# Two decoder layers on one core: layer norms applied by ScalarE, layer 1's weight products made at the start, and a planner with a priority for every operation

## The chip, the cores and the metric

The kernel runs on one core of a Trainium2 chip. A core has five engines with queues of their own: TensorE (PE in the profile; its weight loads are shown apart as PEld), VectorE (DVE), ScalarE (ACT), GpSimd (POOL) and SyncE (SP), which here issues all DMAs. Every engine takes its instructions strictly in the order in which the program lists them; a wait at the head of a queue holds everything behind it.

The metric is the device time of one execution in microseconds (us), lower is better. The time before is 2389.19 us, the median of three runs (2387.06 to 2392.53).

## The reference

The input is `x` of 64 x 64 x 256 in float32 (4096 tokens of width 256, in 64 sequences of 64) and a context `ctx` of the same shape. Two layers of three blocks each are applied, each block to a layer norm of `x`, and its result is added to `x`:

```python
x = x + L0_attn(layernorm(x), ...)      # 16 heads of 128, 4 key heads, norm of q and k, rotary, causal
x = x + L0_xattn(layernorm(x), ctx, ctx) # 32 small heads of 8 channels, no causal mask
x = x + L0_ffn(layernorm(x), ...)       # dense layer plus one of 8 rank-16 experts
x = x + L1_attn(layernorm(x), ...)      # 16 heads of 16, one key head
x = x + L1_xattn(layernorm(x), ctx, ...) # 16 heads of 128, q and k normed by their rms over 2048
x = x + L1_ffn(layernorm(x), ...)       # gated, with 8-bit rounding of inputs and weights
```

Products that need more than half precision are made from a high and a low float16 part of each operand, in three matmuls (high x high, high x low, low x high).

## The kernel before

**Tiles and groups.** Tokens are worked on in 16 groups of 256 (`GT`). A group's `xt` is a tile of 128 partitions x 2 x 256. In phase a, a group goes through layer 0: `l0_attn`, `l0_xattn`, `l0_ffn`, and is stored to DRAM (`mid`); in phase b it is loaded again and goes through layer 1: `l1_attn`, `l1_xattn`, `l1_ffn`. Several groups are in flight at once, and the first groups of phase b overlap the last ones of phase a.

**How the order is made.** The functions don't emit instructions. They record operations with `s.o(engine, cost, reads, writes, fn)`, or with `s.alt`, where one of several engines may be taken. `Sched.plan` then simulates the engines with the recorded costs and picks, one by one, the operation to place next: among those that can start earliest (within `EPS`), the one with the smallest due time. A due time is the time at which the operation would run if its group ran alone, stretched and spaced by `PACE`, plus an offset by the name of the tile that it writes (`LEAD`). `tmin` is an earliest time, `after` adds a dependence, `WINDOW` limits how many groups of each phase are in flight, `SPACE` spaces the score matmuls of cross attention. Tiles come from pools (`COUNTS`): 8 PSUM banks (`B`), 67 tiles of 2 KB per partition (`k2`), 6 of 4 KB (`k4`) and so on; an operation is placed only when its buffers are free. The list so made is emitted, and the chip then runs each engine's part in that order, whatever the real durations are.

**Layer norm** (`layer_norm`, L530 to L548). DVE takes mean and variance (`ln_st`, `ln_mv`), POOL adds the epsilon and a scale and raises to the power -1/2 (`ln_rs`), and DVE applies it to each of the two halves of 256 columns as (x - mean) * rs, into `xh`. The factor `XS` = 16 is folded into rs. There are six per group, 96 in all.

**Layer 0's cross attention** takes `xh` times 16; `stack_rows` (L949) splits it into high and low parts scaled by 4/16 (ACT L955, DVE L956), stores them to DRAM and reads them back in another arrangement into `Q`, a part of a fixed tile named `ovl`. Score matmuls (`xs_ps` L1009, `xt_ps` L1043) work on 32 rows each; ACT takes the exponentials (`xpt` L1050), and PE multiplies by the values (`xo_ps` L1059); `xot_ps` (L1071) and `yo` (L1087) turn the result back.

**Setup for layer 1's cross attention** is recorded after phase a's group 1 with `tmin` = 150 us (in `net`), so it lies amid phase a. `gram_setup` (L1326), called for the q and for the k weights, makes W transposed times W in eight pieces of 256 rows: for each piece and each half of the columns, PE writes its own bank `g_ps` (L1343; the bias product in one column, L1345), and DVE adds the bank to `g_G` (L1350). `value_out_setup` (L1375) multiplies value and output weights of each head into `n_ps` (L1392), stores them to DRAM, finds a scale over all of them, loads them again, splits them into high and low and stores those. `l1_xattn_load` (L1484) loads the split weights (`x1wki`, `x1wq`, `x1wn`, 32 tiles of 2 KB) for phase b; it gives three of eight weights a dependence on layer 0's attention of group 14, and the other five on that of group 15. `l1_attn_setup` is recorded with the first setups, with `tmin` = 70 us.

**Layer 1's cross attention** makes its norms from the gram matrix (`gy_ps`), the projections `qk_ps` in `proj2` (L412 to L414), scores `s_ps` (L1632), values `vn_ps` (L1511) and the output `acc` (L1534).

## Time and profile before

| | us |
|---|---|
| median of three runs | 2389.19 |
| profiled execution, its own time | 2390.41 |
| profiled execution, span of the page | 2388.5 |
| PE busy | 2169.8 |
| DVE busy | 1948.4 |
| POOL busy | 1630.4 |
| ACT busy | 1516.3 |

The mean granted TensorE clock is 0.961 of full speed. The span counts from the first to the last instruction. A busy share is an average over stages that differ: the page also gives each engine's busy share in forty slices, with the TensorE clock in each, and those are to be read before the averages. In a row of the groups of instructions stand the line, the engine, the operation, what is written and read, the shapes and the count; then the busy time in us, the mean duration of one in ns, and the engine's idle time just before them with what ended it. Matmuls overlap one another, so the mean duration of one is longer than the time that it adds. A row of waits gives who waited for whom, the total in us, how often, and the longest.

### The profile page before, as it was taken

The numbers are of one execution on the slowest core, as the hardware profiler recorded it, in microseconds if no ns is written. First come the engines' busy times: TensorE is split into PE (matmuls) and PEld (weight loads), VectorE is DVE, ScalarE is ACT, GpSimd is POOL, SyncE is SP. The second block draws the span as 40 slices with busy tenths as digits, with TensorE's granted clock in tenths as the row PEclk, the third lists the DMA queues.
The fourth block names the chain that finished last, engine by engine and source line by source line (L and its number), as shares of the span: only waits on it lengthen the run. The fifth ranks groups of instructions, "written<-read, shape, count | busy, mean of one in ns | idle before, by whom it ended". The sixth has DMA issues, their size and how long they took to land. (4 is left out here: it accounts for less than half of the span.)

```text
span 2388.5 us, 69732 instructions
## 1 busy us (share of the span) xinstructions
PE 2169.8 (91%) x28232; PEld 1701.9 (71%) x28232; DVE 1948.4 (82%) x4532; ACT 1516.3 (63%) x2843; POOL 1630.4 (68%) x1572
## 2 busy tenths in 40 slices
PE   3499999888999898898878999999999999999996
PEld 2387666655566565665544779898999898899995
DVE  7768788898797889898988867887888888888767
ACT  6475666877878676777557565565556565566542
POOL 5899668777787577767645466767777666666632
PEclk9699999999999998999977999999999999999997
DMA  5243234444355333433464353343444334444321
GB/s 182 74 88 91 59 83 107 125 129 103 87 136 136 108 92 83 129 97 80 111 158 108 57 118 72 76 80 73 86 82 80 76 76 81 81 86 77 59 42 28
DMA packets 484323, 220.83 MB, mean 92 GB/s; under 512 B 340568, under 2 KB 463384, under 8 KB 484000
## 3 DMA queue, kind: packets, MB, share of 16 engines
q1 hardware_dynamic: 484000, 216.37, 39.9%
q8 instruction: 222, 3.64, 0.6%
q14 instruction: 101, 0.83, 0.1%
HBM read 89.06 MB, written 34.64 MB: 52 GB/s over the span
## 5 line engine op out<-in xcount | busy, mean ns | idle before, releaser
L1050 ACT ACTIVATE xpt<-xt_ps,xes 128x512 f32<-128x512 f32 x512 | 313.2, 698 | 75.5 <-PE xt_ps L1043 71.7
L1511 PE MATMUL vn_ps<-x1wn,cTs 128*64 128x256 f16 x6144 | 354.1, 274 | 0.0
L1511 PEld LDWEIGHTS <-cTs 128*64 128x64 f16 x6144 | 332.1, 110 | 8.4 <-issue 6.2
L1016 DVE TENSOR_REDUCE xmx<-xs_ps 128x2 f32<-128x512 f32 x512 | 317.2, 679 | 18.1 <-PE xs_ps L1009 17.4
L1518 DVE SCALAR_TENSOR_TENSOR vn<-vn_ps,vn 128x512 f16<-128x512 f32 x256 | 174.5, 684 | 96.9 <-ACT vn L1516 96.4
L1516 ACT ACTIVATE vn<-vn_ps 128x512 f16<-128x512 f32 x256 | 151.9, 595 | 159.3 <-PE vn_ps L1511 157.5
L604 POOL TENSOR_TENSOR s<-s,sm_mx 128x1024 f32<-128x1024 f32 x96 | 184.7, 1924 | 78.8 <-DVE sm_mx L603 71.4
L633 POOL TENSOR_TENSOR phl<-s,phl 128x512 f16<-128x512 f32 x192 | 223.6, 1176 | 12.3 <-ACT phl L632 10.3
L630 POOL TENSOR_TENSOR s<-s,sm_sm 128x512 f32<-128x512 f32 x192 | 199.5, 1056 | 4.7 <-POOL sm_sm L623 0.3
L1059 PE MATMUL xo_ps<-xpt,xve 128*32 128x256 f32 x2048 | 165.0, 414 | 7.1 <-DVE s L1291 4.9
L815 POOL TENSOR_TENSOR qu<-qu,sw 128x512 f32<-128x512 f32 x128 | 165.5, 1304 | 2.0
L813 POOL TENSOR_TENSOR sw<-sw,rp0s 128x512 f32<-128x512 f32 x128 | 165.3, 1304 | 2.2 <-ACT sq L811 1.6
L810 ACT COPY sw<-q_ps 64x512 f32<-64x512 f32 x256 | 148.0, 580 | 28.1 <-PE q_ps L414 18.8
L632 ACT CAST phl<-s 128x512 f16<-128x512 f32 x192 | 118.2, 622 | 73.7 <-POOL s L630 70.8
L1761 POOL TENSOR_TENSOR gu<-gu 128x704 f32<-128x704 f32 x32 | 55.0, 1721 | 138.2 <-ACT sig L1759 129.9
L1620 ACT ACTIVATE k<-qk_ps,x1kb 128x256 f32<-128x256 f32 x242 | 101.4, 471 | 72.6 <-PE qk_ps L414 67.3
L412 PE MATMUL q_ps<-xT,l0w 128*128 128x256 f16 x512 | 139.8, 273 | 3.7 <-ACT sw L810 1.8
L412 PE MATMUL acc<-l0w,ohl 128*128 128x256 f16 x512 | 141.7, 277 | 0.6 <-ACT sw L810 0.2
L413 PE MATMUL acc<-l0w,ohl 128*128 128x256 f16 x512 | 141.4, 276 | 0.0
L414 PE MATMUL acc<-l0w,ohl 128*128 128x256 f16 x512 | 141.3, 276 | 0.0
L412 PE MATMUL qk_ps<-cTs,x1wki 128*128 128x256 f16 x512 | 140.3, 274 | 0.0
L412 PE MATMUL qk_ps<-xT,x1wq 128*128 128x256 f16 x512 | 139.7, 273 | 0.2 <-DVE xmx L1016 0.2
(414 smaller groups left out, 6666.4 us busy)
## 6 DMA issues: line engine op xcount, KB each, us to landing
ovl<-hl_d SPq DMA_DIRECT2D x96, 128.0 KB
vx<-vt SPq DMA_DIRECT2D x64, 128.0 KB
ctx<-in_ctx_dram SPq DMA_DIRECT2D x32, 256.0 KB
hl_d<-hl SPq DMA_DIRECT2D x64, 128.0 KB
wd<-w_hl SPq DMA_DIRECT2D x32, 256.0 KB
q1st<-q_d SPq DMA_DIRECT2D x128, 64.0 KB
xt<-in_x_dram SPq DMA_DIRECT2D x16, 256.0 KB
ctx_a<-in_ctx_dram SPq DMA_DIRECT2D x8, 512.0 KB
```

What stands on the lines that cost most here:

```text
L412: nc.tensor.matmul(out, lh, rh, start=(st and i == 0), stop=False, **kw)
L604: s.o("POOL", 1900, [mx], [s1], lambda m, t: nc.gpsimd.tensor_tensor(t, t, bc(m, 2, 64), ALU.subtract))
L630: s.o("POOL", 1030, [sm], [s1.sub(j)], lambda m, t, h=h: nc.gpsimd.tensor_tensor(t[:, h], t[:, h], bc(m[:, h], 2, 64), ALU.mult))
L633: s.alt([("POOL", c_pool(482), lambda t, _, p, h=h: nc.gpsimd.tensor_tensor(pl(p, 1), t[:, h], pl(p, 0), ALU.subtract)), ("DVE", c_dves(51 ...
L813: s.o("POOL", 1225, [sg], [sw], lambda t, w: nc.gpsimd.tensor_tensor(v(w), v(w), bc(t, 1, 8), ALU.mult))
L815: ("POOL", 1225, lambda w, d: nc.gpsimd.tensor_tensor(view(d), view(d), w, ALU.add))], [sw], [dt])
L1016: nc.vector.tensor_reduce(m[:, h, bs % 4, :], p, AX.X, ALU.max))
L1050: nc.scalar.activation(t, p, AF.Exp, scale=a))
L1059: nc.tensor.matmul(o[32 * hh:32 * hh + 32, hs, :], v[:, n, a:a + 32], r[hh][:, n, :], start=(n == 0 and hs == 0), stop=(n == 1), skip_grou ...
L1511: nc.tensor.matmul(r[-1][64 * h:64 * h + 64, p, :], x[:, b // 2, a, k, t], w.part(r, c, 2 * (2 * p + h) + k), start=(n == 0), stop=(n == 5))
L1516: nc.scalar.activation(v(t), p, AF.Copy, scale=2.0 ** -15))
L1518: nc.vector.scalar_tensor_tensor(v(l), p, 2.0 ** -15, v(h), ALU.mult, ALU.subtract))
```

## The change

The change has these parts.

1. `layer_norm`: POOL makes -mean * rs for each half (`ln_nb`), and ACT applies the norm as x * rs + nb, in place of DVE.
2. Layer 0's cross attention asks for its norm times 4, so that `stack_rows` splits it without a scale: a plain copy on ACT or DVE, and a subtraction on POOL or DVE.
3. `gram_setup` accumulates all eight pieces in two PSUM banks, computes the second half's columns 128 to 256 only, and reads the banks once at the end. Its pieces, and the value-out products (split off into `value_out_products`), get earliest times from 5 us on, 3 us apart, in place of 150 us on, 15 us apart.
4. `l1_attn_setup` moves to the setups recorded after group 1, with `tmin` = 150 us.
5. `l1_xattn_load`: the eight weights depend on layer 0's attention of groups 12, 12, 13, 14, 15, 15, 15, 15.
6. The planner: an offset for every operation of a group by its place (`FINE`), a penalty in due time for a change of PE tiling (`HOLD`), new values of `LEAD`, `EPS`, `PEN`, `SPACE`, `SHIFT`, `PACE`, and 8 groups of phase b in flight for 6. A test that holds PSUM banks back for operations that need more than two of them is added with a bound (`RESV`) so high that it never applies. Some recorded costs change, and the zeroing of `Q` and `K` may go to DVE.

The diff, without the tables of `LEAD` and most of `FINE`:

```diff
-HOLD = 0
+HOLD = 1026
...
             for o, t in zip(ops, memo[ph]):
                 o.due += base + t * stretch
+            for i, n, v in FINE[ph]:
+                for o in ops[i:i + n]:
+                    o.due += v
...
+                if len(need.get("B", ())) > 2:
+                    wide.append((o, est))
...
-            for k in cands:
+            for k in [k + (1,) for k in cands] + cands:
                 o, need = k[4], k[7]
+
+                if len(k) > 10 and k[5] == "PE" and "B" in need and any(
+                        q is not o and q.due + RESV < o.due and t <= k[9] for q, t in wide):
+                    continue
...
     xh = s.T("k2", [128, 2, D], name="xh")
+    nb = s.T("sm", [128, 2], name="ln_nb")
     for j in range(2):
-        s.o("DVE", c_dve2(D, 2), [xt, mv, rs], [xh.sub(j)], lambda x, m, r, h, j=j: nc.vector.tensor_scalar(
-            h[:, j, :], x[:, j, :], m[:, j, 0:1], r[:, j:j + 1], ALU.subtract, ALU.mult))
+        s.o("POOL", 170, [mv, rs], [nb.sub(j)], lambda m, r, b, j=j: nc.gpsimd.tensor_scalar(
+            b[:, j:j + 1], m[:, j, 0:1], r[:, j:j + 1], -1.0, ALU.mult, ALU.mult))
+    for j in range(2):
+        s.o("ACT", c_act(D, 2), [xt, nb.sub(j), rs], [xh.sub(j)], lambda x, b, r, h, j=j: nc.scalar.activation(
+            h[:, j, :], x[:, j, :], AF.Identity, scale=r[:, j:j + 1], bias=b[:, j:j + 1]))
     return xh
...
     for t in w.q + w.k:
-        s.o("POOL", 2000, [], [t], lambda t: nc.gpsimd.memset(t, 0.0))
+        s.alt([("POOL", 2000, lambda t: nc.gpsimd.memset(t, 0.0)),
+               ("DVE", 1130, lambda t: nc.vector.memset(t, 0.0))], [], [t])
...
-    if isinstance(scale, float):
-        s.o("ACT", c_act(512), [src], [hl.sub(0)], lambda x, h: nc.scalar.activation(h[:, 0], x, AF.Copy, scale=scale))
-        s.o("DVE", c_dves(512), [src, hl.sub(0)], [hl.sub(1)], lambda x, h0, h: nc.vector.scalar_tensor_tensor(
-            h[:, 1], x, scale, h[:, 0], ALU.mult, ALU.subtract))
+    if scale is None:
+        s.alt([("ACT", c_acts(512), lambda x, h: nc.scalar.copy(h[:, 0], x)),
+               ("DVE", c_dve2(512), lambda x, h: nc.vector.tensor_copy(h[:, 0], x))], [src], [hl.sub(0)])
+        s.alt([("POOL", c_pool(482), lambda x, h0, h: nc.gpsimd.tensor_tensor(h[:, 1], x, h[:, 0], ALU.subtract)),
+               ("DVE", c_dves(512), lambda x, h0, h: nc.vector.tensor_tensor(h[:, 1], x, h[:, 0], ALU.subtract))],
+              [src, hl.sub(0)], [hl.sub(1)])
...
-    xh = layer_norm(e, xt)
-    stack_rows(e, xh, 4.0 / XS, Q, ((0, 0), (1, 0), (2, 1)))
+    stack_rows(e, layer_norm(e, xt, 4.0), None, Q, ((0, 0), (1, 0), (2, 1)))
...
+    pa, pb = s.T("B", [128, 258], name="g_ps"), s.T("B", [128, 129], name="g_ps")
     for q in range(8):
         t = s.T("k4", [128, 2, 257], name="g_w")
...
-        for h in range(2):
-            ps = s.T("B", [128, 258], name="g_ps")
...
-            s.o("PE", 1108, [t], [ps], f)
...
-        s.tmin += STEP[0]
+        def f(t, a, b, q=q):
+            for k in range(2):
+                kw = dict(stop=(q == 7 and k == 1), skip_group_check=True)
+                st = q == 0 and k == 0
+                nc.tensor.matmul(a[:, 0:257], t[:, k, 0:128], t[:, k, :], start=st, **kw)
+                nc.tensor.matmul(b, t[:, k, 128:256], t[:, k, 128:257], start=st, **kw)
+                nc.tensor.matmul(a[:, 257:258], t[:, k, 256:257].to_broadcast([128, 128]), t[:, k, 256:257],
+                                 start=False, **kw)
+        s.o("PE", 1600, [t], [pa, pb], f)
+        s.tmin += STEP[2]
...
+    def f(a, b, g, bb):
+        nc.vector.tensor_copy(g[:, 0, 0:128], a[:, 0:128])
+        nc.vector.tensor_scalar(g[:, 0, 128:257], a[:, 128:257], 2.0, None, ALU.mult)
+        nc.vector.tensor_copy(g[:, 1, 128:256], b[:, 0:128])
+        nc.vector.tensor_scalar(g[:, 1, 256:257], b[:, 128:129], 2.0, None, ALU.mult)
+        nc.vector.tensor_scalar(bb, a[:, 257:258], 1.0 / 2048, 1e-6, ALU.mult, ALU.add)
+    s.o("DVE", 850, [pa, pb], [g, w.bb], f)
...
-def value_out_setup(e, I):
+def value_out_products(e, I):
...
+    t0 = s.tmin
+    s.tmin = STEP[3]
     w.gq = gram_setup(e, I, "gram_q")
     w.gk = gram_setup(e, I, "gram_k")
+    value_out_products(e, I)
+    s.tmin = t0
...
-        s.after = after[i > 2]
+        s.after = after[i]
...
-SPACE = (7898, 3165)
+SPACE = (7280, 2713)
 BURST = 1
-SHIFT = 2276.53
+SHIFT = -45512.85
...
-PACE = dict(a=(77726.07, 2.1), b=(72833.37, 2.08))
-STEP = (15e3, 60e3)
-WINDOW = (5, 6)
+PACE = dict(a=(77722.93, 2.1), b=(69870.52, 2.04))
+STEP = (15e3, 60e3, 3e3, 5e3)
+WINDOW = (5, 8)
...
+            if "a1" in sb:
+                l1_attn_setup(e, I)
             if "x1" in sb:
                 l1_xattn_setup(e, I)
...
-            l1_xattn_load(e, [e.done.get(("a0", max(g, 0))) for g in (ng - 2, ng - 1)])
+            l1_xattn_load(e, [e.done.get(("a0", max(ng - k, 0))) for k in (4, 4, 3, 2, 1, 1, 1, 1)])
```

## The prediction

> **What bounds the kernel now.** I read the page's busy shares first, then its forty slices, then the same by stage, and last the waits inside the stages that lose most.
>
> ```profile
> span 2388.5 us, 69732 instructions
> PE 2169.8 (91%) x28232; PEld 1701.9 (71%) x28232; DVE 1948.4 (82%) x4532; ACT 1516.3 (63%) x2843; POOL 1630.4 (68%) x1572
> PE   3499999888999898898878999999999999999996
> PEclk9699999999999998999977999999999999999997
> ```
>
> PE leads, but not evenly: two poor slices at the start, 8s and 9s through layer 0, a dip with a low clock around slices 20 to 22, then full until the end. The stretches 0-120 (filling), 120-1140 (layer 0 in full swing), 1140-1380 (layer 0 runs out, layer 1 begins), 1380-2340 (layer 1) and the rest give, in the view of busy time by stretch (PE, PEld, DVE, ACT, POOL, then the granted clock):
>
> ```profile
> 0.00:120.00 120.00, 50.20 (x399) 36.05 (x400) 89.47 (x228) 63.24 (x125) 86.43 (x95) 0.80 0.42 128
> 120.00:1140.00 1020.00, 937.81 (x10618) 658.07 (x10616) 866.08 (x2014) 740.18 (x1335) 782.19 (x701) 0.98 0.41 102
> 1140.00:1380.00 240.00, 200.82 (x2293) 124.52 (x2292) 203.70 (x466) 145.49 (x283) 126.86 (x129) 0.86 0.46 105
> 1380.00:2340.00 960.00, 954.17 (x14632) 863.54 (x14632) 755.86 (x1746) 559.16 (x1092) 623.68 (x638) 1.00 0.40 77
> 2340.00:2388.50 48.50, 26.78 (x302) 19.68 (x296) 33.34 (x80) 8.19 (x12) 11.19 (x12) 0.73 0.14 33
> ```
>
> PE idles 69.8, 82.2, 39.2, 5.8 and 21.7 us there: 218.7 in all. Layer 1 has nothing left to give; a change gains at the start, in layer 0 or at the hand-over, or by taking work off PE. In layer 0 PE (92%) and DVE (85%) are close, ACT (73%) and POOL (77%) are not far.
>
> **The start.** PE's first waits are for the scales of layer 0's weights, and the first projection begins when the first transposed group lands:
>
> ```profile
> PE am_ps L441 <- DVE w_am L501: 31.1, 4, 16.8
> 33.63 0.39 PE L412 MATMUL v_ps<-l0w,xT 128*128 128x256 f16 x1 [3.76 <-DMA xT<-xhl]
> ...
> 30.38 1.35 SPq L556 DMA_TRANSPOSE xT<-xhl  x1
> ```
>
> **The hand-over.** The issue times of the loads of layer 1's prepared weights on SP, and the first product that uses them:
>
> ```profile
> 1161.16 2.01 SPq L1490 DMA_DIRECT2D x1wq<-wd  x4
> ...
> 1237.30 1.86 SPq L1490 DMA_DIRECT2D x1wq<-wd  x4
> ...
> 1247.83 3.39 SPq L1490 DMA_DIRECT2D x1wn<-wd  x4
> ...
> L412 PE MATMUL qk_ps<-cTs,x1wki x512: 269/273/421, 1300.1 to 2303.4; 128*128 128x256 f16 x171
> ```
>
> Layer 0's last self attention ends near 1245 and layer 1's first big product starts at 1300; between them PE has little but cross attention.
>
> **The rows that carry prices:**
>
> ```profile
> L1343 PE MATMUL g_ps<-g_w 128*128 128x257 f32 x128 | 35.3, 397 | 1.4 <-DVE qu L812 1.4
> L1345 PE MATMUL g_ps<-g_w 128*128 128x1 f32 x64 | 8.0, 229 | 0.0
> L1392 PE MATMUL n_ps<-n_o,n_v 128*128 128x256 f32 x64 | 15.7, 385 | 2.7 <-DMA n_v<-in_x_viT_dram 2.2 <-DVE s L913 0.5
> L547 DVE TENSOR_SCALAR xh<-xt,ln_mv,ln_rs x192: 312/406/2444, 19.8 to 2361.1; 128x256 f32<-128x256 f32 x192
> L956 DVE SCALAR_TENSOR_TENSOR hl<-xh,hl 128x512 f16<-128x512 f32 x16 | 14.4, 901 | 0.0
> L1350 DVE TENSOR_TENSOR g_G<-g_G,g_ps 128x257 f32<-128x257 f32 x32 | 13.1, 415 | 5.5 <-PE g_ps L1345 4.2 <-PE g_ps L1343 1.0
> L1258 ACT ACTIVATE q<-q_ps,a1b,a1u x32: 767/816/841, 1191.4 to 2183.9; 128x256 f32<-128x256 f32 x32
> ```
>
> **Step A: weight products first.** All gram and value-out matmuls ran between 120 and 1140: 35.3 + 8.0 + 15.7 = 59.0 us of PE. In the changed program's PE order all 96 gram entries and all 32 value-out entries stand ahead of the first po product, amid the first projections: in the stretch where PE idles 69.8. The gram is cheaper too. Of 128 wide passes half stay (17.6 us), half shrink to 129 columns (64 at about 165 ns, from xot_ps L1071, 256 in 42.3 us: 10.6), the one-column ones stay (8.0): 36.2 for 43.3. So 51.9 us goes into 69.8 idle, and 59.0 leaves layer 0.
>
> It isn't free. On SP's queue the first transposition moves from behind 24 DMAs (5.6 MB) to behind 54: twenty 256 KB weight pieces, 15 gram pieces, 4 of ctx_a, 5 of x and 6 value-out pieces, 14.2 MB; several wait for PE or ACT to free a buffer. The stretch 5 to 15 us moved 344 to 352 GB/s, so 14.2 MB lands at 44 us at the earliest; with the 3.3 us from 30.38 to 33.63 the first projection starts at 47, not 33.6: 13 late at least. Buffer waits I put at 5 more: 18 late. Everything of layer 0 that is queued on PE behind it starts as late. Net: 18 - 59 = **-41**. Ends: -46 (13 late) and +10 (40 late, and only half of the 59 counted because layer 0 isn't held by PE alone).
>
> Layer 1 attention's own setup leaves the start as well; its PE wait (am_ps for nr_y, 7.7 us) is counted at 0, since the next product, rk, came ready only 0.2 us later.
>
> **Step B: norms on ACT, and the new order of layer 0.** 55.4 us of DVE (the 102 xh of 120 to 1380) and the 16 hl (14.4) and 32 g_G (13.1) leave DVE: 83 of its 1070 us there. ACT takes the xh: 102 at 0.47 (k L1620, one operand by pointer) to 0.82 us (L1258 above, two; the nearer form), so 48 to 83 on 886. POOL takes 16 hl at 1.17 (xhl L568) and about 102 products of 128x1 at 0.21 (L541): 40 on 909. All three then stand near 76 to 78%. What PE gets of it no row shows: at best the 82.2 + 39.2 idle falls by half, -60. At worst each norm's chain grows by two POOL steps and the slower pair, 2 x 0.21 + 2 x (0.82 - 0.54), about 1 us, bare for all 48 norms of layer 0: +48. The priorities by operation and the wider window reorder the same work; the longest listed PE wait in this stage is 4.1 us, so they can only nibble. I take **-20**, nearer to the idle that DVE's share explains (121 x 83/1070 = 9) than to half. In layer 1, cover is ACT's own idle time (401 us of 960) against 84 xh x 0.82 = 69: 0.
>
> The Trainium skill ("ScalarE: Activation LUTs", rules for kernel authors) speaks against this step: elementwise add and multiply belong on VectorE, and an ACTIVATE takes some 0.3 us plus 0.83 ns an element, so an estimated 0.51 us here. By that price ACT takes 52 us in these stages, and the sum stays as it is. L547's 312/406/2444 says why the ranking may not hold here: DVE's mean is 541 beside a busy POOL.
>
> **Step C: hand-over.** The loads are released two and three groups earlier (behind layer 0's attention of groups 12, 12, 13, 14 and 15 instead of 14 and 15). On PE, qk_ps follows the last acc of layer 0 at once; before, 382 entries lay between. Entries of layer 1 (qk, vn, acc) ahead of the last yo grow from 432 to 888, entries of cross attention behind the first qk from 276 to 401. The idle is 39.2, and a clock of 0.86 over 240 us hides at most 33.6 more. I take **-25**, about a third; ends 0 and -53.
>
> **Step D.** Layer 1 is full and the same matmuls run: 0. The tail (21.7 idle behind the last xqT and hqT transpositions) keeps its chain: 0, two norm steps dearer at most (+1).
>
> **Sum.** -41 - 20 - 25 = -86 on the profiled execution's 2390.4 (span 2388.5 and 1.9 around it): 2304. That run is 1.2 above the median, so **2303**.
>
> **The rivals.**
> *Layer 0 isn't held by PE.* Its groups (62 to 64 us each) could be paced by the chain through POOL and DVE, as 85% and 77% hint; then only half of the 59 counts (18 - 30 = -12) and B gives 9 alone: -12 - 9 - 25 = -46, 2343. Against it: PE at 92%, no listed wait over 4.1 us.
> *Early loads choke layer 0* (the change does not do what it is for): 32 of 67 2 KB buffers are held some 120 us longer, so fewer groups are in flight. Price: the starved pace of 1200 to 1260, 13.9 idle in 60, for 120 us: +28 in place of -25, 2356.
> *Slower: ACT stuck behind POOL.* Each xh pair waits in ACT's queue for the two nb steps, which stand in POOL's queue behind instructions of up to 1.9 us (s L604). Behind the waiting ACT stand the exponentials that free cross attention's PSUM, and in layer 1 vn's evictions, for which PE, with no slack, would stop. It decides from 86/96 = 0.9 us bare per norm; at 1.3 us it costs 125: 2428. For it: ACT already waits 70.8 us on POOL (phl for s). Against it: L547 itself waited only 12.7 us for POOL's ln_rs in 192.
>
> **How the numbers follow.** A measurement of this kernel tells about 0.2% (4.8 us) from no change. My forecast has 0.58 (its own range 2255 to 2335), the half gain 0.20, choked loads 0.08, stuck ACT 0.11, and a cancelling mixture 0.03. Faster then has 0.58 + 0.20 + 0.08 = 0.86, same 0.03, slower 0.11. The range runs from 2245 (A and C at their good ends and B at -40: -139) to 2375, which takes in the half gain and the choked loads and leaves out the slower case.
>
> **What the changed profile would show.** A: gram and value-out matmuls in the first 100 us, the first v_ps near 50, PE idle before 120 down by 30 or so, none of them after 140. B: xh under ACT near 0.5 to 0.8 us, DVE under 81% in layer 0, PE idle per 60 us of layer 0 below 4.8. C: x1w loads from about 1000 on, the first qk_ps within 10 us of the last layer-0 acc, clock there above 0.9. I am wrong if v_ps starts after 75, if ACT's waits for ln_nb pass 90 us, or if layer 1's PE is no longer full.

## The result, and the profile after

The changed kernel takes 2412.52 us (median of four runs, 2409.14 to 2416.93) against 2388.12 for the kernel before beside it: a ratio of 1.010, with a 95% interval of 1.0078 to 1.0122. It is 24 us slower; 86 faster was forecast. The profiled execution took 2411.24 us, with a span of 2409.5.

The page of the changed kernel, its head and PE's forty slices with the granted clock:

```profile
span 2409.5 us, 69823 instructions
PE 2160.3 (90%) x28232; PEld 1701.7 (71%) x28232; DVE 1844.2 (77%) x4276; ACT 1589.8 (66%) x3033; POOL 1693.6 (70%) x1780
PE   6894788899988888999979999999999999999996
PEclk8996998999999989999989999999999999999997
```

The start is full (6, 8), but the fourth slice (180 to 240 us) is a 4 with a clock of 0.6, and the 8s of layer 0 are still there. The same by stage, busy time of PE, PEld, DVE, ACT and POOL, then the clock:

```profile
0.00:120.00 120.00, 87.05 (x513) 72.46 (x514) 62.88 (x196) 77.65 (x171) 65.91 (x87) 0.86 0.74 218
120.00:1140.00 1020.00, 876.41 (x10141) 603.53 (x10140) 808.05 (x1872) 733.00 (x1327) 803.24 (x767) 0.93 0.38 93
1140.00:1380.00 240.00, 209.55 (x2678) 144.09 (x2675) 188.54 (x450) 175.70 (x330) 154.60 (x168) 0.93 0.42 100
1380.00:2340.00 960.00, 941.13 (x14248) 842.93 (x14248) 737.59 (x1657) 583.78 (x1175) 646.93 (x732) 1.00 0.40 76
2340.00:2409.50 69.50, 46.21 (x665) 38.66 (x662) 47.12 (x105) 19.69 (x34) 22.93 (x29) 0.81 0.20 39
```

PE's idle time, each row's length less its busy time, adds up with its busy time to the change of the span:

| stage, us | PE idle before | after | difference |
|---|---|---|---|
| 0 to 120 | 69.8 | 33.0 | -36.8 |
| 120 to 1140 | 82.2 | 143.6 | +61.4 |
| 1140 to 1380 | 39.2 | 30.5 | -8.7 |
| 1380 to 2340 | 5.8 | 18.9 | +13.1 |
| the rest | 21.7 | 23.3 | +1.6 |
| PE busy | 2169.8 | 2160.3 | -9.5 |
| sum | | | +21.1 |

So the weight products did fill the start, and layer 0 gave back more than that. Cut once at 400 us, the stage of 120 to 1140 shows where, first in the kernel before, then in the changed one:

```profile
120.00:400.00 280.00, 266.90 (x2924) 203.25 (x2921) 224.78 (x526) 187.73 (x329) 229.00 (x199) 0.99 0.37 82
400.00:1140.00 740.00, 670.92 (x7696) 454.82 (x7695) 641.30 (x1489) 552.46 (x1008) 553.19 (x503) 0.97 0.43 110
```

```profile
120.00:400.00 280.00, 212.76 (x2321) 145.44 (x2321) 192.33 (x451) 183.14 (x335) 235.46 (x211) 0.85 0.40 105
400.00:1140.00 740.00, 663.65 (x7828) 458.08 (x7824) 615.72 (x1421) 549.86 (x993) 567.77 (x557) 0.97 0.37 88
```

Of the 61.4, 54.1 lie between 120 and 400 us (67.2 for 13.1), and 7.3 behind it. Before, the gram products stood in just that stretch:

```profile
L1343 PE MATMUL g_ps<-g_w x128: 377/381/484, 162.8 to 397.6; 128*128 128x257 f32 x128
```

The start and this stretch together (0 to 400 us) lost 17.3 us: what was filled in front opened again behind.

Three rows of the changed kernel's timeline, two of POOL and one of PE, show how layer 0 begins (start, duration, engine, line, operation; in brackets the idle time ahead and what ended it):

```profile
13.57 0.73 POOL L554 TENSOR_TENSOR ln_rs<-ln_mv,mhalf 128x2 f32<-128x2 f32 x1
...
55.13 1.42 POOL L558 TENSOR_SCALAR ln_nb<-ln_mv,ln_rs 128x1 f32<-128x1 f32 x1 [1.04 <-DVE l0eps L788]
...
68.81 0.40 PE L422 MATMUL v_ps<-l0w,xT 128*128 128x256 f16 x1 [1.04 <-DMA xT<-xhl]
```

The first group's `ln_rs` is there at 14.30, its `ln_nb` begins 41 us later, and the first projection starts at 68.81 in place of 33.63. Then PE's waits from 120 to 300 (who waited for whom, total, times, longest):

```profile
PE xs_ps L1025 <- DMA ovl<-hl_d: 25.8, 1, 25.8
PE xo_ps L1075 <- ACT xpt L1066: 4.4, 3, 3.0
```

The first cross attention alone waits 25.8 us. Its `hl` stands on POOL and ACT behind layer 1's weight blocks, whose product `w_x1ki` waits on POOL for the load of `w_n`; POOL's waits of the same stretch have it first:

```profile
POOL w_x1ki L1481 <- DMA w_n<-in_nki_s_dram: 7.4, 1, 7.4
```

At the hand-over, in the views by tile, layer 0's last acc product and layer 1's first `qk_ps` follow each other at once, at 1286.9 and 1287.0:

```profile
L424 PE MATMUL acc<-l0w,ohl x512: 271/273/421, 151.2 to 1286.9; 128*128 128x256 f16 x171
```

```profile
L422 PE MATMUL qk_ps<-cTs,x1wki x512: 269/273/284, 1287.0 to 2337.4; 128*128 128x256 f16 x171
```

The norm's new operations (min, median and max in ns), and how long ACT stood idle for the first of them:

```profile
L558 POOL TENSOR_SCALAR ln_nb<-ln_mv,ln_rs x192: 257/267/1415, 55.1 to 2380.6; 128x1 f32<-128x1 f32 x192
L561 ACT ACTIVATE xh<-xt,ln_nb,ln_rs x192: 583/599/682, 58.6 to 2381.2; 128x256 f32<-128x256 f32 x192
...
  POOL ln_nb L558: 38.2, 34
```

In layer 1 (1400 to 2300 us, some fourteen groups) PE now waits where it didn't before: eleven times for ACT's `v`, up to 0.7 us each, and eight times for `pT`:

```profile
PE vn_ps L1533 <- ACT v L1258: 7.8, 11, 0.7
PE ctx L1319 <- DMA pT<-phl: 5.4, 8, 1.2
```

**Milestones.** Three times cut the run: the start of the last acc product (96 to a group) of layer 0's first group, that of its sixteenth group, and the end. Before: 151, 1245, 2388.5. After: 176, 1287, 2409.5. So the first group is 25 later, the sixteen groups take 1111 for 1094 (+17), and what comes behind them 1122.5 for 1143.5 (-21).

These sections compare kernels as they stand only where the same work lies between the milestones. Between the two orders it doesn't: by the first milestone PE has begun 1125 matmuls in the changed kernel and 685 before, and from the last one on 16081 and 16351 are left. PE's idle time in the three sections says more: 69.8, 104.5 and 44.5 us before, 35.9, 163.1 and 50.1 after. So the -21 at the end is 27 us less PE busy time and 6 us more idle time: work done ahead of the milestone, or at a higher clock, and no wait saved.

Within the sixteen groups the loss stands at the front. The start of the last acc product of the first, second, fifth and sixteenth group, with the same of four experiments that follow:

| kernel | 1st | 2nd | 5th | 16th | 1st to 5th | 5th to 16th |
|---|---|---|---|---|---|---|
| before | 151 | 210 | 408 | 1245 | 257 | 837 |
| changed | 176 | 288 | 470 | 1287 | 294 | 817 |
| b_prod | 231 | 289 | 487 | 1318 | 256 | 831 |
| b_double | 151 | 214 | 432 | 1276 | 281 | 844 |
| a_late | 177 | 276 | 479 | 1301 | 302 | 822 |
| a_dve | 175 | 286 | 469 | 1300 | 294 | 831 |

The changed kernel loses 37 us up to its fifth group and gains 20 behind it. From the first to the second group it takes 112 us for 59. In the kernels of the next section's table, those that start from the changed one take 99 to 132 there, and those that start from the kernel before 57 to 63. What in the new order does this was not found.

### The profile page after: what moved, and what is told of

It is laid out like the page before. It is cut to its first block, busy times and chain, and to the rows that moved or that the text cites. A ratio compares the mean times of both kernels' runs of the same rounds, so it can differ in the third digit from the quotient of the medians.

```text
span 2409.5 us, 69823 instructions
## 1 busy us (share of the span) xinstructions
PE 2160.3 (90%) x28232; PEld 1701.7 (71%) x28232; DVE 1844.2 (77%) x4276; ACT 1589.8 (66%) x3033; POOL 1693.6 (70%) x1780
## 4 chain that ended last, share of the span: by engine, by line
PE 47%; POOL 15%; DVE 13%; ACT 9%; DMA 8%; issue 7%; SPq 2%; POOLq 0%; ACTq 0%; DVEq 0%
PE vn_ps L1533 12%; PE qk_ps L422 4%; PE qk_ps L423 4%; PE qk_ps L424 4%; ACT xpt L1066 3%; DVE xmx L1032 3%; PE acc L1556 3%; POOL sw L827 2%; POOL phl L647 2%; PE xo_ps L1075 2%; POOL qu L829 2%; POOL s L644 2%; PE s_ps L1654 2%; DMA pT<-phl 2%; PE gu_ps L1776 1%
## 5 line engine op out<-in xcount | busy, mean ns | idle before, releaser
L644 POOL TENSOR_TENSOR s<-s,sm_sm 128x512 f32<-128x512 f32 x192 | 205.0, 1083 | 5.5 <-POOL sm_sm L637 0.2
L829 POOL TENSOR_TENSOR qu<-qu,sw 128x512 f32<-128x512 f32 x128 | 165.5, 1301 | 2.8 <-POOL s L929 0.7
L1075 PE MATMUL xo_ps<-xpt,xve 128*32 128x256 f32 x2048 | 147.9, 403 | 8.4 <-ACT xpt L1066 6.8
L422 PE MATMUL q_ps<-xT,l0w 128*128 128x256 f16 x512 | 142.7, 279 | 3.6 <-DVE xmx L1032 1.9
L423 PE MATMUL q_ps<-xT,l0w 128*128 128x256 f16 x512 | 141.9, 277 | 0.0
L424 PE MATMUL q_ps<-xT,l0w 128*128 128x256 f16 x512 | 141.7, 277 | 0.0
## 6 DMA issues: line engine op xcount, KB each, us to landing
ovl<-hl_d SPq DMA_DIRECT2D x96, 128.0 KB
vx<-vt SPq DMA_DIRECT2D x64, 128.0 KB
hl_d<-hl SPq DMA_DIRECT2D x64, 128.0 KB
```

What stands on the lines that cost most here:

```text
L422: nc.tensor.matmul(out, lh, rh, start=(st and i == 0), stop=False, **kw)
L423: nc.tensor.matmul(out, lh, rl, start=False, stop=False, **kw)
L424: nc.tensor.matmul(out, ll, rh, start=False, stop=(i == n - 1), **kw)
L644: s.o("POOL", 1030, [sm], [s1.sub(j)], lambda m, t, h=h: nc.gpsimd.tensor_tensor(t[:, h], t[:, h], bc(m[:, h], 2, 64), ALU.mult))
L829: ("POOL", 1225, lambda w, d: nc.gpsimd.tensor_tensor(view(d), view(d), w, ALU.add))], [sw], [dt])
L1075: nc.tensor.matmul(o[32 * hh:32 * hh + 32, hs, :], v[:, n, a:a + 32], r[hh][:, n, :], start=(n == 0 and hs == 0), stop=(n == 1), skip_grou ...
```

## Experiments

There are two kinds. Kernels named b_ start from the kernel before, those named a_ from the changed one. Where durations or engines of instructions are edited, the order stays as it was. Where operations are moved, `plan` runs unchanged, and then the list is laid out again by the planned times, some of them altered by `moves`; an operation that depends on a later one follows it, and buffers must be free. Ahead of what is moved the order stays as it was: in b_hand10n, which moves the hand-over, PE's first 11354 matmuls are those of the kernel before. The tables of offsets aren't fitted anew.

The expectations go by names for rival explanations. 'PE-held': PE's work is what layer 0 takes its time for. 'In step': the groups advance at the pace of a chain over all engines, and products only fill gaps of PE. 'Hole': the wait of 25.8 us costs the time. 'Ramp': layer 0's first groups can't fill PE without the products among them. 'Norms': the norm on ScalarE costs it.

All times (median; ratio to the kernel before beside it, with its 95% interval; then, from one profiled execution, first projection, first group's last acc, sixteenth's, sixteen groups, and the rest of the span behind it, to within 1 us). The kernels ran on several chips, each beside the kernel before; between them the ratios are compared:

| kernel | us | ratio | v_ps | first | 16th | 16 groups | rest |
|---|---|---|---|---|---|---|---|
| before | 2388.12 | | 34 | 151 | 1245 | 1094 | 1143.5 |
| changed | 2412.52 | 1.010 (1.0078 to 1.0122) | 69 | 176 | 1287 | 1111 | 1122.5 |
| b_double | 2418.89 | 1.0133 (1.0109 to 1.0156) | 34 | 151 | 1276 | 1125 | 1141 |
| b_prod | 2456.86 | 1.0285 (1.0256 to 1.0313) | 41 | 231 | 1318 | 1087 | 1140 |
| b_nb | 2393.18 | 0.9997 (0.9982 to 1.0011) | 34 | 153 | 1249 | 1096 | 1142 |
| b_act | 2420.99 | 1.0136 (1.0120 to 1.0153) | 34 | 152 | 1263 | 1111 | 1156.5 |
| b_actv | 2415.42 | 1.0103 (1.0088 to 1.0118) | 35 | 153 | 1270 | 1117 | 1144 |
| b_act0 | 2402.97 | 1.0053 (1.0034 to 1.0072) | 35 | 153 | 1260 | 1107 | 1141 |
| a_dve | 2430.11 | 1.0180 (1.0160 to 1.0200) | 69 | 175 | 1300 | 1125 | 1126 |
| a_sm1 | 2416.97 | 1.0111 (1.0096 to 1.0126) | 41 | 183 | 1291 | 1108 | 1126 |
| a_late | 2425.83 | 1.0130 (1.0113 to 1.0147) | 69 | 177 | 1301 | 1124 | 1126 |
| a_loads | 2431.60 | 1.0183 (1.0158 to 1.0208) | 68 | 199 | 1307 | 1108 | 1127 |
| a_prod | 2437.06 | 1.0208 (1.0180 to 1.0237) | 64 | 170 | 1308 | 1138 | 1127 |
| a_nohand | 2467.89 | 1.0320 (1.0296 to 1.0343) | 69 | 177 | 1292 | 1115 | 1175 |
| b_hand10n | 2424.91 | 1.0134 (1.0102 to 1.0166) | 34 | 152 | 1252 | 1100 | 1172 |
| b_hand20n | 2441.65 | 1.0196 (1.0173 to 1.0218) | 34 | 151 | 1266 | 1115 | 1171 |
| b_hand30 | 2406.99 | 1.0072 (1.0046 to 1.0098) | 34 | 152 | 1257 | 1105 | 1147 |

### What is PE's work in layer 0 worth? (b_double, b_prod)

b_double issues every weight product twice at its place:

```diff
-                for k in range(2):
+                for _ in range(2):
+                  for k in range(2):
                     nc.tensor.matmul(p[:, 0:257], ...)
...
-                for c in range(2):
+                for c in (0, 1, 0, 1):
                     nc.tensor.matmul(p[:, c, :], ...)
```

> The kernel before in its own order, with every gram and value-out matmul issued twice at its place (the second overwrites the first): 59 us more PE work between 120 and 1140. Theory 'PE-held': 45 to 60 us slower. Theory 'in step': 5 to 25 slower, with PE idle in 120 to 1140 falling from 82.2 to about 40.

The sixteen groups became 31 us longer and the run 30, 24 of the 31 up to the fifth group. The work added is less than the 59.0 that the rows of these products sum to, since the rows overlap: by the page PE is busy for 43.4 us more than the 2169.8 before.

```profile
PE 2213.2 (92%) x28488; PEld 1743.5 (72%) x28488; DVE 1946.6 (81%) x4532; ACT 1515.8 (63%) x2843; POOL 1629.0 (67%) x1572
```

PE's row from 120 to 1140:

```profile
120.00:1140.00 1020.00, 955.32 (x10593) 680.16 (x10591) 838.91 (x1962) 713.83 (x1289) 757.02 (x680) 0.98 0.39 99
```

Idle time fell from 82.2 to 64.7. So layer 0 is neither held by PE alone nor free of it: a microsecond of PE work added in these places costs 0.5 (of 59) to 0.7 (of 43.4). Both theories missed, 'in step' by 5 us, and with 64.7 us idle where it had forecast about 40.

b_prod takes the products out of layer 0 and puts them in front:

```diff
+    # gram pieces 0 to 15, value-out pieces 16 to 23, and all that belongs to them
+    at[o] = 5e3 + 3e3 * i + max(0.0, min(o.start - t0, 12e3))
```

> The kernel before in its own order, except that all 24 weight-product pieces and what belongs to them stand at 5 to 75 us of its plan, 3 us apart, in place of 150 to 745: the first part of the change alone. Theory 'PE-held' (the prediction's: PE work taken out of layer 0 is time gained): first projection at 45 to 60 in place of 34, but layer 0's last self attention ends 25 to 45 us earlier, and the run is 20 to 40 faster, at 2348 to 2368. Theory 'in step' (layer 0's groups advance at the pace of a chain over all engines, and the products only fill gaps of PE): layer 0 ends as much later as it starts, the gaps stay as PE idle in 120 to 1140 (82.2 before, above 110 here), and the run is 5 to 30 slower.

The sixteen groups gained 7 us (1087 for 1094) with all these products gone from among them: PE is busy for 30 us less there and idle for 24 us more (128.0 for 104.5). Up to the fifth group, where the gram products had stood, nothing is gained (256 for 257). The first group ended 80 us later, though its first projection began only 7 later. PE's idle time in 120 to 1140 is 134.2, the late start included:

```profile
0.00:120.00 120.00, 76.15 (x373) 60.57 (x374) 56.85 (x184) 43.84 (x92) 51.97 (x66) 0.80 0.46 138
120.00:1140.00 1020.00, 885.85 (x9870) 610.43 (x9870) 821.64 (x1909) 705.33 (x1270) 754.81 (x676) 0.94 0.38 95
```

So where the work goes, the gap stays, and taking work out brings less than adding it costs. That the loss at the start is that of a crude layout and not the price of the idea is argued; the pace of the sixteen groups is what this run shows.

### What does the norm on ScalarE cost? (b_nb, b_act, b_actv, b_act0, a_dve)

Four kernels keep the order of the kernel before. b_nb adds only POOL's small products and uses none of them; b_act applies every norm on ScalarE with the product on POOL; b_actv has the product on VectorE; b_act0 is b_act for layer 0 alone.

```diff
 # b_act; b_actv has nc.vector in the first line
+            nc.gpsimd.tensor_scalar(m[:, j, 0:1], m[:, j, 0:1], r[:, j:j + 1], -1.0, ALU.mult, ALU.mult)
+            nc.scalar.activation(h[:, j, :], x[:, j, :], AF.Identity, scale=r[:, j:j + 1], bias=m[:, j, 0:1])
-            nc.vector.tensor_scalar(h[:, j, :], x[:, j, :], m[:, j, 0:1], r[:, j:j + 1], ALU.subtract, ALU.mult)
```

> The kernel before in its own order, except that every norm's last step is done on ScalarE, with the two small POOL products straight ahead of it. Theory 'norms': slower by 15 to 25 us, with PE idle rising in layer 0 and in layer 1. Theories 'ramp' and 'hole': within 8 us of the kernel before either way.

> The kernel before in its own order and with its norms on VectorE, plus only the two small POOL products of every norm (their result is not used). With the norms on ScalarE this order was 33 us slower. If POOL's new steps are what costs there: 15 to 30 slower. If ScalarE's longer step and the handing over POOL to ScalarE cost: within 10 of the kernel before.

> The kernel before in its own order with the norm's last step on ScalarE, but the small product ahead of it on VectorE in place of POOL. Theory 'handing over' (ScalarE waits behind POOL's queue: 94.2 us in 58 waits with the product on POOL, 33 us slower): most of the loss goes, the run is 0 to 12 slower than the kernel before. Theory 'ScalarE's step' (0.6 us on an engine whose queue carries the evictions of PSUM): the loss stays at 22 to 35.

> The kernel before in its own order with the norms on ScalarE (small products on POOL) in layer 0 alone, layer 1's on VectorE. By the milestones of the run with all norms on ScalarE (18 us lost by the sixteenth group's last acc, 13 after it): 15 to 21 slower than the kernel before. If layer 0's lag is taken up by layer 1's slack or its own: below 10.

The 192 products on POOL cost nothing that can be measured (0.9997). The norms on ScalarE cost 33 us in that order (1.36% of 2389), although DVE, the second busiest engine, lost 55 us of them in layer 0. By the milestones 18 are lost by the sixteenth group and 13 behind it. Layer 0's norms alone cost 12 in the run and 15 by its sixteenth group. The product is written into `ln_mv` here. In the views of the norm's tile, ACT's idle time ahead of it (what ended it, us, times), first of b_act, then of b_actv:

```profile
  POOL ln_mv L548: 94.2, 58
```

```profile
  DVE ln_mv L548: 89.6, 57
```

ACT waits about as long whichever engine makes the product. In layer 1, though, the engine matters. PE's row of 1380 to 2340, of b_act and then of b_actv:

```profile
1380.00:2340.00 960.00, 944.80 (x14280) 845.62 (x14274) 706.85 (x1654) 597.23 (x1183) 649.14 (x729) 1.00 0.40 76
```

```profile
1380.00:2340.00 960.00, 953.74 (x14508) 856.02 (x14508) 731.03 (x1755) 607.52 (x1197) 632.51 (x648) 1.00 0.41 78
```

15.2 us of idle time with the product on POOL, 6.3 with it on VectorE; before it was 5.8. So layer 1's 13 us come with handing over from POOL (with the product on VectorE 1 us is left there), and layer 0's 15 to 25 with the norm on ScalarE in an order planned for VectorE, whichever engine makes the product. That other instructions behind the waiting one on ACT are what layer 0 pays for is argued, not shown.

a_dve goes the other way, in the order of the changed kernel: the small products go, and VectorE applies the norms.

> The changed kernel's own order, except that every norm's last step is issued on VectorE from mean and reciprocal deviation, as before the change, at the same place of the order; the two small POOL steps go. Theory 'norms': faster by 15 to 25 us, layer 1's PE waits for ACT's v fall from 7.8 us, and PE idle in 1380 to 2340 falls from 18.9 to about 6. Theories 'ramp' and 'hole': 0 to 15 slower, since DVE gets about 104 us of work back and PE's idle time stands elsewhere; the wait of 25.8 us at the first cross attention stays.

It is 0.8% slower than the changed kernel, the first five groups take as long (294), and layer 1 doesn't get better:

```profile
1380.00:2340.00 960.00, 939.28 (x14193) 838.37 (x14188) 803.17 (x1772) 543.36 (x1090) 629.33 (x651) 1.00 0.39 77
```

Here an order fitted to one engine lost when the work went to another, in both directions. What norms on VectorE would give in an order fitted to them and to the other parts isn't told by this.

### The late start and the first gap (a_sm1, a_late, a_loads, a_prod)

`ln_nb` is a new tile of the smallest pool, which has ten buffers, and in the planned order, which no trace shows, hardly any of them is free from 12 to 58 us. a_sm1 gives the layout 15 (and one buffer of 1 KB fewer, to make room) and moves the first group's operations:

```diff
+MORE = dict(sm=15, k1=5)
+    return {o: o.start - 28e3 for o in ops if o.grp == 0 and 50e3 <= o.start < 140e3}
```

> The changed kernel's own order, with 15 of the smallest buffers in place of 10, and only the first group's operations of 50 to 140 us of the plan standing 28 us earlier (the preceding try moved all groups, and the layout lost the overlap of layer 1's groups, which says nothing of the start). If the missing small buffer holds the first projection: it starts at 35 to 50 in place of 69 and the first group's last acc ends by 166 in place of 176. If the run is paid by the start: 5 to 20 us faster than the changed kernel (2393 to 2407). If later groups do not take it up: within 6 of the changed kernel, or slower.

The first projection comes 28 us earlier:

```profile
40.71 0.39 PE L493 MATMUL v_ps<-l0w,xT 128*128 128x256 f16 x1 [4.75 <-DMA xT<-xhl]
```

So the buffer held it: a_prod2, which also asks for the groups 28 us earlier but keeps ten buffers, has its first projection at 62.5, and a_sm2, with fifteen, at 40.8. But the first group's last acc comes no earlier (183 for 176) and the run isn't faster. The group takes 142 us from its first projection to its last acc, against 118 before. The run can't tell what an earlier projection is worth, however: only operations planned at 50 to 140 us were moved, and the first group's last acc stayed behind the same 1125 matmuls of PE as in the changed kernel.

a_late moves the preparation of layer 1's four weight blocks 60 us later, to take away the wait of 25.8 us; a_loads moves the loads of the first block 40 us earlier instead:

```diff
+    block = st[nm.index("w_x1ki0"):nm.index("n_am1")]          # a_late
+    return {o: o.start + 60e3 for o in block}
...
+    return {o: o.start - 40e3 for o in ops if o.grp == 15.5 and o.eng == "SP"   # a_loads
+            and not o.deps and 150e3 <= o.start < 162e3}
```

> The changed kernel's own order, except that the preparation of layer 1's four key, value and query weight blocks (loads, POOL products, splits; 155 to 393 us of the plan) stands 60 us later. Theory 'hole': the wait of 25.8 us for the first cross attention goes, PE busy in 180 to 240 rises from 25.7 to above 40, and the run is 12 to 25 us faster than the changed kernel, at 2387 to 2400. If the wait is covered by slack of the following groups: PE busy in 180 to 240 rises, but the sixteenth group's last acc (1287) moves by less than 8 and the run is within 8 of the changed kernel.

> The changed kernel's own order, except that the loads of layer 1's first prepared weights, which its plan puts at 150 to 162 us, stand 40 us earlier in the plan. Theory 'hole' (one wait costs the time: POOL's product w_x1ki stands 7.4 us for the load of w_n, and behind it on POOL, ACT and DVE stands the first group's cross attention, for which PE waits 25.8 us): PE busy in 180 to 240 rises from 25.7 to above 40 and the time falls by 15 to 25 us, to 2388 to 2398. Theory 'ramp' (layer 0's first groups cannot fill PE once the weight products are gone from among them): the wait moves elsewhere in 180 to 300, and the time falls by less than 8. Theory 'norms' (the norm on ScalarE is what costs): less than 5 either way.

In a_late the gap shrinks, by its row of 180 to 240 and its waits:

```profile
180.00:240.00 60.00, 40.02 (x432) 28.95 (x433) 46.23 (x109) 28.34 (x52) 50.48 (x46) 0.74 0.33 91
```

```profile
PE xs_ps L1100 <- DMA ovl<-hl_d: 16.7, 2, 14.3
```

PE is busy for 40.0 us in place of 25.7, and yet the sixteenth group ends 14 us later and the run is no faster (1.0130 against 1.0100). The groups show why this doesn't settle the theory of the gap. The second group ends 12 us earlier than in the changed kernel (276 for 288), as the longest wait is 11.5 shorter; the fifth ends 9 later (479 for 470), and PE's idle time from 400 to 700 is 41.4 for 29.0. So the second group did gain the wait, and it was lost again by the groups behind it, among which the moved block now stands; that the block is the reason is argued. a_loads left 17.6 us of the wait and held up the first group by 23 us, since the loads stand ahead of its transfers; it doesn't tell the theories apart.

a_prod spreads the changed kernel's products over 110 to 300 us:

```diff
+    at = {o: 110e3 + 8e3 * i + min(o.start - t0[i], 9e3) for o, i in piece.items()}
```

> The changed kernel's own order, except that the 24 weight-product pieces (16 of the gram, 8 value-out) and what belongs to them are spread over 110 to 300 us of the plan, 8 us apart, in place of 5 to 75. Theory 'ramp': the first projection starts near 35 in place of 69, PE idle in 120 to 300 falls from 52 to below 30, and the time falls by 20 to 40 us, to 2373 to 2393. Theory 'hole': the wait of 25.8 us stays and only the start moves, 0 to 12 faster. Theory 'norms': within 5.

The first projection started at 64, not near 35, because its `ln_nb` kept its place (54.5), and the first group ended 6 earlier (170). PE's idle time from 120 to 300 fell to 36.5 from 52.1, not below 30, but the second group came 13 later (301 for 288) and the sixteen groups took 28 longer, so the theory of the ramp found no gain of time in it. Three tries that moved all groups against the setup, a_prod2 (2540.48 us), a_sm2 (3394.62) and a_smlate (3363.32), lost the overlap between groups in the layout; their times say nothing of their questions, and only the first projections are used above:

> The changed kernel's own order, except that the weight products are spread over 110 to 300 us of the plan and all groups of both layers stand 28 us earlier against the setup. If the late start of layer 0 (35 us) is what the change pays for its full first stage: first projection at 35 to 45, PE idle in 0 to 120 back near 70, in 120 to 300 below 35, and the run 15 to 35 faster than the changed kernel, at 2378 to 2398. If any move away from the planned order costs more than it brings: 10 or more slower than the changed kernel.

> The changed kernel's own plan, but the pool of the smallest buffers (256 bytes a partition, 10 in the plan) has 15 when the order is laid out again, and all groups of both layers stand 28 us earlier against the setup; the weight products stay in front. Reading to be tested: the first group's ln_nb stands on POOL at 55.13, though its ln_rs was there at 14.30, because the new tile ln_nb found no free small buffer in the plan, and not because PE was busy with the products. If so, the first projection starts at 35 to 50 in place of 69, the first group's last acc ends 10 to 25 us earlier than 176, and if layer 0 keeps its pace (1111 us from the first group's last acc to the sixteenth's) the run is 8 to 22 us faster than the changed kernel, at 2390 to 2404. If the products on PE hold the first projection instead, it starts at 60 or later and the run is within 8 of the changed kernel or slower.

> Both of the two preceding edits together. If start and hole both cost the run their full size: 25 to 45 us faster than the changed kernel, at 2367 to 2387, level with the kernel before or ahead of it. If only one counts: as that one alone. If neither: within 10 of the changed kernel or slower.

### The hand-over (a_nohand, b_hand30, b_hand20n, b_hand10n)

a_nohand undoes the early hand-over in the changed kernel, the others bring it into the kernel before:

```diff
+    # a_nohand: +60e3 and +30e3; b_hand30, b_hand20n, b_hand10n: -70e3 and -30e3, -20e3, -10e3
+    at = {o: o.start + 60e3 for o in ops if o.eng == "SP" and name_of(o).startswith("x1w")}
+    at.update((o, o.start + 30e3) for o in ops if o.grp >= 16)
```

> The changed kernel's own order, except that layer 1's groups stand 30 us and the loads of its prepared weights 60 us later against layer 0: the third part of the change undone. If the hand-over is worth its step: the first qk_ps comes 10 to 30 us later than 1287, PE idle in 1140 to 1380 rises from 30.5 to above 40, and the run is 10 to 25 us slower than the changed kernel. If layer 1's early work only takes turns with layer 0's last groups: within 8 of the changed kernel.

> The kernel before in its own order, except that the loads of layer 1's prepared weights stand 70 us earlier in the plan and all of layer 1's groups 30 us earlier against layer 0's: the hand-over alone. If the hand-over is worth what the prediction put on it: PE idle in 1140 to 1380 falls from 39.2 to below 28, the granted clock there rises from 0.86 to above 0.9, and the run is 10 to 30 us faster. If layer 1's early work only gets in the way of layer 0's last groups on every engine: the first qk_ps moves 15 to 40 earlier, layer 0's last cross attention ends later, and the run is within 8 of the kernel before or slower.

> The kernel before in its own order, layer 1's groups 10 us earlier against layer 0's and the loads of its prepared weights 70 us earlier. Undone in the changed kernel, the early hand-over cost 55 us; with 30 us of shift in the kernel before it brought a loss of 16. If a smaller shift lets layer 1's first products in without holding up layer 0's last groups: 3 to 12 us faster than the kernel before (2378 to 2386), the first version ahead of both. If the order of the kernel before has no room for it: 0 to 10 slower.

> As the preceding edit, with 20 us. If the gain grows with the shift: 5 to 20 us faster than the kernel before. If layer 1's early operations stand in the queues of layer 0's last groups: 5 to 15 slower, the sixteenth group's last acc later than 1245 by 5 or more.

Undone, it costs some 53 us (1.0320 against 1.010); the first `qk_ps` moves to 1325.9. Its row of 1140 to 1380, and that of b_hand10n:

```profile
1140.00:1380.00 240.00, 191.16 (x2104) 117.85 (x2100) 159.23 (x378) 153.60 (x282) 130.07 (x144) 0.86 0.35 89
```

```profile
1140.00:1380.00 240.00, 184.62 (x2019) 111.91 (x2017) 178.40 (x410) 124.93 (x245) 109.80 (x110) 0.85 0.43 104
```

But shifts of 10, 20 and 30 us in the kernel before, with the loads 70 us earlier, cost 31, 47 and 18 (b_hand30 also keeps the planner's test that holds buffers back for older groups, the other three count free buffers alone). Whether they lose because the layout is stirred at all, or because the early loads hold buffers that layer 0's last groups need, isn't told apart. But where a move of 10 us costs 31, the 53 of a_nohand can't be read as the worth of the hand-over, and the other a_ kernels with moved operations carry the same doubt. None of the versions tried beats the kernel before.

## Why the prediction was wrong

**Step A, weight products first: -41 forecast.** What it said of the start held: idle time fell by 36.8 ("down by 30 or so"), and all products ran early. The term that failed is "59.0 us leaves layer 0", counted as time gained. As an amount it was too large, since it adds rows that overlap: doubling the products made PE busy for 43.4 us more. And as a gain it hardly came: 30 us were lost by doubling, but only 7 gained in the sixteen groups by taking the products out (b_prod), and none up to the fifth group, where the gram had stood. In the changed kernel PE's idle time rose by 54.1 us from 120 to 400, more than the start had gained, and the first five groups took 37 us longer; behind them 20 came back. The part of the new order that costs those 37 us is not known: they stay when the norms go back to VectorE (a_dve), and b_prod, with the products in front in the old order, doesn't have them. The start was sized wrongly as well: the first projection was 35 late, not 18, and for another reason than SP's queue, a missing small buffer. What that lateness costs isn't shown. The two ends of the step, -46 and +10, were not wide enough: the upper end still gave half of 59.

**Step B, norms on ACT: -20 forecast.** The prices were nearly right (0.47 to 0.82 us forecast, 0.60 measured; 0.21 for POOL's product, 0.27 measured; DVE at 79% in layer 0, under the 81% named). What PE gets of it was taken from a share of busy time, and the sign was wrong: in the order of the kernel before the same step costs 33 us. "PE idle per 60 us below 4.8" came out as 8.4 (143.6 in 17 stretches). The Trainium skill's rule that spoke against this step ("ScalarE: Activation LUTs", rules for kernel authors: adds and multiplies belong on VectorE) points the way of the 33 us, and the row that was held against it, DVE's mean of 541 ns, was no reason; a_dve's 18 us, lost by going back, point the other way. The 0.51 us estimated from the same rules was short of the 0.60 measured. How much of the changed kernel's 24 us is due to the norms is open, for in its own order taking them back costs 18 us too.

**Step C, hand-over: -25 forecast.** The marks held: the first `qk_ps` 0.1 us behind the last acc, a clock of 0.93, the first loads at 1049. The gain isn't to be seen: PE's idle time fell by 8.7 us from 1140 to 1380, but from 1140 to the end it rose from 66.7 to 72.7, and the 21 us that are missing behind the sixteenth group are work done ahead of it or at a higher clock. What the earlier loads gave, apart from the new order as a whole, isn't shown. By the trace 471 matmuls lay between the two products before, where the prediction counts 382 entries.

**Step D, layer 1: 0 forecast.** Idle time there grew by 13.1, with PE waiting for ACT's `v` and for `pT`. The cover that the step named, ACT's 401 us of idle time, doesn't help an instruction that stands in line at the wrong moment; b_act and b_actv showed 8.9 us between two engines for a product of 0.27.

**The rivals.** "Layer 0 isn't held by PE" was right that PE's work doesn't set the pace; whether the chain through POOL and DVE does isn't shown. Its half is what b_double measured for work added; for work taken out b_prod gave 7 us. And it kept a gain for B and for the hand-over in full. "ACT stuck behind POOL" had the right side and the nearest number (2428). Its mark, ACT waits for `ln_nb` above 90 us, was not reached (38.2); it was in b_act (94.2), at 33 us slower. The nearness is luck: 2428 is 86 us of gains that didn't come and 125 of waits that didn't either. Of the three signs of being wrong, only the last came, PE idle for 18.9 us in layer 1, and 13.1 more than before.

**What stays open.** The +25, +17 and -21 are measured, but the three parts of the change can't be priced one by one from these runs: each part was planned with the others. Plans with tables of offsets fitted to one part alone were not made. The 2245 of the range is 5 below what its three good ends give (2250).

## What to carry to other kernels

Where four in-order engines are each busy for some three quarters and more, work taken off the busiest one can be worth a fraction: double it in place, and take it out, before counting its removal in full. Here doubling cost 30 us, and removal gave 7. A wait or a late start that stands out in the trace isn't yet a cost: follow milestones (the last product of every group), and count what work is done by each, since a new order can put other work ahead of the same milestone. An order fitted to one assignment of engines can lose a per cent when an operation changes engine, even towards a less busy one, so a change of engine and a new order are one decision, and are measured together.

## What the runs showed of the hardware

- The clock goes with the gap: in 180 to 240 us it was 0.63 with PE busy for 25.7 us (changed kernel), 0.68 with 42.3 (a_prod), 0.74 with 40.0 (a_late), 0.86 with 51.7 (b_prod), and 1.00 with 56.6 (b_nb). The work within such a stretch is slower: of its half-precision matmuls of 128x256, 273 ns in the median, 22 of 101 took over 400 ns in the changed kernel, and none of 312 in the kernel before.
- 192 instructions of 128x1 on POOL, 0.31 us each in the median, cost no measurable time (b_nb: 0.9997, 0.9982 to 1.0011), but the same products as the last thing that ScalarE waits for cost 8.9 us of PE time in layer 1 against VectorE's.
- A norm's half of 128x256 takes 0.60 us on ScalarE (583 to 682 ns) and 0.41 on VectorE in the median, there with single ones up to 2.44 us.
